# A convolution layer and an eight-expert network: routing by chunks of 2048 tokens, the network in 135 picked units between the convolution's tiles

## The chip, the cores and the metric

The kernel runs on one core of one Trainium2 chip. The metric is the device time of one execution in microseconds, lower being better. The kernel before takes 4087.13 us (median of 3 runs, 4083.84 to 4097.9).

## The reference

Input `x` has 8 images of 256 channels and 64 by 64 pixels, all in float32. A convolution layer is followed by a layer of experts; both add to their input.

```python
# x = x + conv(_ln_c(x));  t = tokens(x);  t = t + ffn(_ln_t(t))
y = depthwise 3x3 of 9 experts; moe = silu(sum_e scale[e,c] * y[e,c] + bias[c])
out = silu(t2 * (w_out @ moe) + shift)
...
idx = argmax(softmax(x @ gate_w + gate_b))        # one expert of 8 for each token
pos = (cumsum(one_hot, axis=0) * one_hot).sum(-1) - 1
kept = pos < C                                    # C = 5120, from 1.25 * 32768 / 8
buf = zeros((E, C, D)).at[idx, pos_safe].set(x, mode='drop')
hmid = relu(einsum('ecd,edf->ecf', buf, w1) + b1) # 256 -> 1024
ybuf = einsum('ecf,efd->ecd', hmid, w2) + b2      # 1024 -> 256
y_tok = ybuf[idx, pos_g] * (prb * kept)[:, None]
y = nan_to_num(y_tok)
```

There are T = 32768 tokens (one for each pixel) and 8 x 5120 = 40960 slots. A token's position is its rank among all tokens of the same expert in the order of the tokens, so a slot is known only when all earlier tokens have been routed. The nine depthwise kernels of a channel collapse to one 3x3 kernel, which both versions compute on the chip (`keff`).

## The kernel before

The kernel is written with a tile framework: it names buffers from pools, and the framework puts the waits in and decides the order of the instructions on each engine's queue. Each engine works through its queue in order. DMAs are issued from the queues of SP (most loads and stores), ACT (the output) and POOL (indirect ones). The kernel has three phases, one behind the other.

**Phase 1** goes over 64 pixel tiles of 512 pixels (8 to an image; 256 channels are two halves of 128 partitions). `norm_stats` and `norm_apply` normalise over channels an image ahead. `conv_taps` makes the 3x3 convolution: TensorE takes four taps as matmuls with diagonal weights (L318), VectorE adds the other five in place in PSUM (L326). `conv_out` is the 1x1 convolution (L340), silu on ACT (L347) and the residual on POOL (L354). `to_tokens` transposes to token-major, writes the tokens to `x_d` in DRAM and computes the gate's logits (L373). Once an image (4096 tokens) is complete, `route_image` turns logits into slots with a chain of small VectorE operations and running counts. `scatter` then writes (token, probability) into the slot table `tab_d` with 32 indirect DMAs from POOL (L474), 128 rows of 8 bytes each. They write the same DRAM tensor, and each waits for the one before it.

**Phase 2** starts when the slot table is complete. It goes over the 8 experts and all 40 slot tiles of 128 of each, whether used or not, in 80 groups of four. For a group it gathers the tokens by the table (L551, POOL), normalises them (L560 to L566), transposes, runs 256 -> 1024 (L587) and 1024 -> 256 (L607) on TensorE, adds the bias on VectorE (L616), multiplies by the probability on ACT (L617), replaces non-finite values (L626 to L633, with POOL's L628) and stores to `y_d`. The weights of an expert, two loads of 1 MB, are loaded once (L541, L543).

**Phase 3** goes over the 64 tiles again: it loads the tokens (L645), gathers the outputs with four indirect DMAs of 128 rows (L651, POOL), adds, transposes back (L664) and stores the result (L673).

Of the kernel before, what the change touches and what calls it, by code (L numbers as in the profile page):

```python
# [8 lines left out]
F32 = mybir.dt.float32  # L9
I32 = mybir.dt.int32  # L10
# [4 lines left out]
DRAM = bass.MemoryType.DRAM  # L15

# [5 lines left out]
# Depthwise taps that the tensor engine takes (diagonal weights); the vector engine adds the rest.  # L22
PE_TAPS = (0, 1, 2, 3)
DVE_TAPS = (4, 5, 6, 7, 8)
# [3 lines left out]
def metaformer_kernel(  # L28
# [26 lines left out]
    NE = w_experts.shape[0]  # conv experts  # L55
# [3 lines left out]
    CAP = max(1, -(-5 * T // (4 * E)))  # ceil(1.25 * T / E)  # L59
    NT = CAP // P  # slot tiles of an expert; slot pos = p * NT + j  # L60
    assert C == D == 2 * P and CAP % P == 0 and w_experts.shape[2:] == (3, 3)
    PX = 512  # pixels of a tile
    RT = PX // W  # image rows of a tile
    NPT = HW // PX  # pixel tiles of an image
    AHEAD = 4  # pixel tiles that loads run ahead of the first use
    NJ = PX // P  # token tiles of a pixel tile
    NIT = HW // P  # token tiles of an image
    NSLOT = E * CAP

    x_v = x.rearrange("b (c p) h w -> b p c (h w)", p=P)  # L70
    out_v = out.rearrange("b (c p) h w -> b p c (h w)", p=P)

    const = ctx.enter_context(tc.tile_pool(name="const", bufs=1))
    dram = ctx.enter_context(tc.tile_pool(name="dram", bufs=1, space=DRAM))

    x1_d = dram.tile([T, C], F32, name="x1_d")  # x after the conv layer, by token
    tab_d = dram.tile([NSLOT, 2], F32, name="tab_d")  # slot -> (token, probability)
    y_d = dram.tile([NSLOT + 1, D], F32, name="y_d")  # expert outputs by slot, then a zero row
# [3 lines left out]
    slots = const.tile([P, B * NIT], I32, name="slots")  # L82

    # The slot table starts at token 0 with probability 0; y_d's last row is 0.
    zeros = const.tile([P, max(NSLOT * 2 // P, D)], F32, name="zeros")
    nc.gpsimd.memset(zeros, 0.0)
    nc.sync.dma_start(
        tab_d.rearrange("(p j) t -> p (j t)", p=P), zeros[:, : NSLOT * 2 // P]
    )
    nc.sync.dma_start(y_d[NSLOT : NSLOT + 1, :], zeros[0:1, :D])  # L90

    b1_sb = const.tile([P, E * NFC], F32, name="b1_sb")

    def rsqrt_eps(dst, var, eps, mhalf):
        nc.gpsimd.tensor_scalar(dst, var, eps, None, ALU.add)
        nc.gpsimd.tensor_tensor(dst, dst, mhalf, ALU.pow)

    # ------------------------------------------------------------------ phase 1
    # Norm over channels, depthwise conv, 1x1 conv, residual, gating, slot table.
    with ExitStack() as ph:  # L100
        wk = ph.enter_context(tc.tile_pool(name="wk1", bufs=1))
        xp = ph.enter_context(tc.tile_pool(name="xp", bufs=18))
        st = ph.enter_context(tc.tile_pool(name="st1", bufs=2))
        io = ph.enter_context(tc.tile_pool(name="io1", bufs=2))
        ps_tr = ph.enter_context(tc.tile_pool(name="ps_tr1", bufs=3, space=PSUM))
        ps_acc = ph.enter_context(tc.tile_pool(name="ps_acc", bufs=3, space=PSUM))
        ps_o = ph.enter_context(tc.tile_pool(name="ps_o1", bufs=1, space=PSUM))
        ps_g = ph.enter_context(tc.tile_pool(name="ps_g", bufs=1, space=PSUM))

        x_tiles = {}  # L110

        def load_x(b, t):
            xt = xp.tile([P, NCC, PX], F32, tag="xt", name="xt")
            nc.sync.dma_start(xt, x_v[b, :, :, t * PX : (t + 1) * PX])
            x_tiles[b, t] = xt

        for t in range(AHEAD):
            load_x(0, t)

        # ---- weights and constants  # L120
        NR = 5 * NE + 4
        rows = wk.tile([NR, C], F32, name="rows")
# [6 lines left out]
        wexp = wk.tile([P, NCC, NE, 9], F32, name="wexp")  # L129
# [3 lines left out]
        wo_sb = wk.tile([P, NCC, C], F32, name="wo_sb")  # L133
        nc.scalar.dma_start(wo_sb, w_out.rearrange("(o p) c -> p o c", p=P))
        wg_sb = wk.tile([P, NCC, E], F32, name="wg_sb")
# [3 lines left out]
        b1_rows = wk.tile([E * NFC, P], F32, name="b1_rows")  # L139
        nc.scalar.dma_start(b1_rows, b1.rearrange("e (f p) -> (e f) p", p=P))  # L140

        mhalf = wk.tile([P, NIT], F32, name="mhalf")
# [3 lines left out]
        cmean = wk.tile([P, P], F32, name="cmean")  # L146
        nc.gpsimd.memset(cmean, 1.0 / C)
        # ntri[k, m] = -1 where k >= m, else 0
# [11 lines left out]
        # erank[e] = E - e  # L160
        erank = wk.tile([P, E], F32, name="erank")
        for e in range(E):
            nc.gpsimd.memset(erank[:, e : e + 1], float(E - e))
        ones_j = wk.tile([P, NIT], F32, name="ones_j")
        nc.gpsimd.memset(ones_j, 1.0)
        count = wk.tile([P, E], F32, name="count")
        nc.gpsimd.memset(count, 0.0)

        par = wk.tile([P, NCC, NR], F32, name="par")
        for c in range(NCC):  # L170
            tr = ps_tr.tile([P, 2, 256], F32, tag="tr", name="tr")
            nc.tensor.transpose(
                tr[:, 0, :NR], rows[:, c * P : (c + 1) * P], ident[:NR, :NR]
            )
            nc.vector.tensor_copy(par[:, c, :], tr[:, 0, :NR])
# [5 lines left out]
        def affine(g, b, m, v, n, name):  # L181
            # t = g * (v + eps)^-0.5, shift = b - m * t
            t = wk.tile([P, NCC, n], F32, name=name + "_t")
            s = wk.tile([P, NCC, n], F32, name=name + "_s")
            mh = wk.tile([P, NCC, n], F32, name=name + "_mh")
            nc.gpsimd.memset(mh, -0.5)
            rsqrt_eps(t, v, BN_EPS, mh)
            nc.vector.tensor_mul(t, t, g)
            nc.vector.tensor_mul(s, m, t)
            nc.vector.tensor_sub(s, b, s)  # L190
            return t, s
# [7 lines left out]
        # The experts' kernels, weighted and summed: one 3x3 kernel per channel.  # L199
# [14 lines left out]
        diag = wk.tile([P, NCC, len(PE_TAPS), P], F32, name="diag")  # L214
        for c in range(NCC):
            for i, k in enumerate(PE_TAPS):
                nc.vector.tensor_scalar(
                    diag[:, c, i, :], ident, keff[:, c, k : k + 1], None, ALU.mult
                )
        woT = wk.tile([P, NCC, C], F32, name="woT")  # L220
        for c in range(NCC):
            tr = ps_tr.tile([P, 2, 256], F32, tag="tr", name="tr")
            for o in range(NCC):
                nc.tensor.transpose(
                    tr[:, 0, o * P : (o + 1) * P],
                    wo_sb[:, o, c * P : (c + 1) * P],
                    ident,
                )
            nc.vector.tensor_copy(woT[:, c, :], tr[:, 0, :C])
        tr = ps_tr.tile([P, 2, 256], F32, tag="tr", name="tr")  # L230
        nc.tensor.transpose(tr[:, 0, : E * NFC], b1_rows, ident[: E * NFC, : E * NFC])
        nc.vector.tensor_copy(b1_sb, tr[:, 0, : E * NFC])
        # (v - mean(v)) @ gate_w = v @ (gate_w - column means of gate_w)
        gm = ps_g.tile([P, NIT * E], F32, tag="g", name="gm")
# [12 lines left out]
        # Normed images with a border of zeros, two in turn.  # L247
        xns = []
        for i in range(2):
            xn = wk.tile([P, NCC, H + 2, W + 2], F32, name=f"xn{i}")  # L250
            nc.gpsimd.memset(xn[:, :, 0 : H + 2 : H + 1, :], 0.0)
            nc.gpsimd.memset(xn[:, :, 1 : H + 1, 0 : W + 2 : W + 1], 0.0)
            xns.append(xn)

        stats = {}

        def norm_stats(b, t):
            xt = x_tiles[b, t]
            mv = st.tile([P, NJ, 2], F32, tag="mv", name="mv", bufs=4)
            for j2 in range(NJ // 2):  # L260
                tr = ps_tr.tile([P, 2, 256], F32, tag="tr", name="tr")
                for jj in range(2):
                    j = 2 * j2 + jj
                    for c in range(NCC):
                        nc.tensor.transpose(
                            tr[:, jj, c * P : (c + 1) * P],
# [3 lines left out]
                for jj in range(2):  # L270
                    s6 = st.tile([P, 6], F32, tag="s6", name="s6", bufs=4)
                    nc.vector.bn_stats(s6, tr[:, jj, :])
                    nc.vector.bn_aggr(mv[:, 2 * j2 + jj, :], s6)
            rs = st.tile([P, NJ], F32, tag="rs", name="rs", bufs=4)
            rsqrt_eps(rs, mv[:, :, 1], LNC_EPS, mhalf[:, :NJ])
            stats[b, t] = mv, rs

        def norm_apply(b, t):
            xn = xns[b % 2]
            xt = x_tiles[b, t]  # L280
            mv, rs = stats.pop((b, t))
            # A transpose of a column spread over 128 columns puts it, as a row, on all
            # partitions.
            bm = ps_tr.tile([P, PX], F32, tag="tr", name="bm")
            br = ps_tr.tile([P, PX], F32, tag="tr", name="br")
            for j in range(NJ):
                nc.tensor.transpose(
                    bm[:, j * P : (j + 1) * P],
                    mv[:, j, 0:1].to_broadcast([P, P]),
# [431 lines left out]
```

## Time and profile before

| what | value |
|---|---|
| runs | 4087.13 us median, 4083.84 to 4097.9 |
| profiled execution: span, first to last instruction | 4073.0 us; no separate time is listed for it, the runs' median is 14.1 us above the span |
| busy: TensorE (PE), VectorE (DVE), ACT, POOL | 85%, 42%, 24%, 35% of the span |
| bytes moved | 273.20 MB, 67 GB/s over the span |
| phase 1 on TensorE | 0 to 1241 us |
| between phases 1 and 2 | 1241 to 1382 us, TensorE busy 0.52 us |
| phase 2 | 1382 to 3708 us, TensorE busy 2297.19 us |
| phase 3 | 3708 to 4073 us, POOL busy 269.54 us |

"PE" is TensorE's matmuls and transposes, "PEld" its weight loads, which overlap. A float32 matmul appears as two instructions in the trace, a transpose as one. "DMA share" is the mean busy share of the core's 16 DMA engines. An engine's idle time is put down to what ended it.

### The profile page before, as it was taken

The page shows a single profiled execution, that of the slowest core. Times are in us where ns is not written, and L with a number is a line of the kernel's source. Part 1 is how long each engine was busy: PE and PEld are TensorE (multiplying, and loading weights), DVE is VectorE, ACT ScalarE, POOL GpSimd, SP SyncE. Part 2 cuts the span into 40 slices and gives each one's busy share as a digit, 9 for nine tenths or more (in the row PEclk, how much of TensorE's full clock was granted, in tenths as well). Part 3 has the DMA queues.
Part 4 walks back from the last instruction along what each step waited for, and adds up shares of the span by engine and source line. Part 5 has one row for each costly group of instructions (what it writes and reads, how often), then busy time and mean ns, then how long its engine had stood idle before and what let it go on. Part 6 is the DMA issues. An engine that isn't in the chain of part 4 may idle for free. (4 is left out here: it accounts for less than half of the span.)

```text
span 4073.0 us, 35799 instructions
## 1 busy us (share of the span) xinstructions
PE 3470.7 (85%) x12971; PEld 2238.5 (55%) x12971; DVE 1724.0 (42%) x3986; ACT 976.3 (24%) x1656; POOL 1438.3 (35%) x1385
## 2 busy tenths in 40 slices
PE   6988888999870499999999999999999999995333
PEld 4554444555440266666666666666666666663232
DVE  7876676777550223232323232333333333322333
ACT  0222122222220123232323232222222222221111
POOL 2244444445433322222222222222222222214776
PEclk9998899999885699999999999999999999997555
DMA  3212121221011111110101111111011111104887
GB/s 111 73 53 57 47 58 52 57 63 37 27 37 49 29 37 38 57 41 32 63 32 42 53 42 45 50 32 63 33 41 56 39 34 39 35 28 156 284 289 272
DMA packets 165972, 273.20 MB, mean 67 GB/s; under 512 B 27058, under 2 KB 102180, under 8 KB 165796
## 3 DMA queue, kind: packets, MB, share of 16 engines
q1 hardware_dynamic: 108194, 160.06, 11.9%
q0 software_dynamic: 35840, 75.81, 6.2%
q10 hardware_dynamic: 21762, 35.05, 2.3%
q8 instruction: 102, 1.67, 0.2%
q14 instruction: 74, 0.61, 0.1%
HBM read 161.20 MB, written 109.64 MB: 66 GB/s over the span
## 5 line engine op out<-in xcount | busy, mean ns | idle before, releaser
L587 PE MATMUL ph_f<-xT,w_sb 128*128 128x512 f32 x2560 | 1121.2, 596 | 23.1 <-ACT xT L582 23.1
L607 PE MATMUL py<-w_sb,hT 128*128 128x256 f32 x5120 | 1118.2, 379 | 0.0
L607 PEld LDWEIGHTS py<-w_sb,hT 128*128 128x128 f32 x5120 | 974.1, 190 | 165.1 <-issue 38.3
L587 PEld LDWEIGHTS ph_f<-xT,w_sb 128*128 128x128 f32 x2560 | 481.0, 190 | 616.3 <-issue 554.6
L551 POOL DMA_INDIRECT xg<-x_d,tab x320 | 319.7, 999 | 1317.8 <-PE tr L577 1238.2
L594 ACT ACTIVATE hT<-ph_f,b_sb 128x512 f32<-128x512 f32 x640 | 439.7, 687 | 642.2 <-PE ph_f L587 642.2
L616 DVE TENSOR_TENSOR v<-py,b_sb 128x256 f32<-128x256 f32 x320 | 121.0, 420 | 1058.0 <-PE py L607 1058.0
L318 PE MATMUL acc<-xn,diag 128*128 128x512 f32 x1024 | 498.2, 628 | 9.3 <-ACT moe L329 9.3
L326 DVE SCALAR_TENSOR_TENSOR acc<-xn,keff,acc 128x512 f32<-128x512 f32 x640 | 444.7, 750 | 57.7 <-PE acc L318 55.4
L474 POOL DMA_INDIRECT tab_d<-dat,slots x256 | 255.9, 1000 | 544.5 <-DMA tab_d<-dat,slots 492.2
L664 PE MATMUL tr<-ident,yt 128*128 128x128 f32 x512 | 120.9, 422 | 244.9 <-issue 159.2
L318 PEld LDWEIGHTS acc<-xn,diag 128*128 128x128 f32 x1024 | 195.2, 202 | 204.3 <-issue 191.6
L651 POOL DMA_INDIRECT yt<-y_d,slots x256 | 269.5, 1053 | 84.4 <-issue 63.1
L340 PE MATMUL po<-moe,woT 128*128 128x512 f32 x512 | 270.9, 653 | 8.7 <-ACT x1c L347 6.9
L617 ACT ACTIVATE v<-v,tab 128x256 f32<-128x256 f32 x320 | 145.1, 502 | 544.9 <-DVE v L616 544.9
L664 PEld LDWEIGHTS tr<-ident,yt 128*128 128x128 f32 x512 | 100.2, 223 | 265.5 <-issue 235.8
L582 ACT COPY xT<-tr 128x512 f32<-128x512 f32 x160 | 92.6, 579 | 621.2 <-PE tr L577 621.2
L560 DVE BATCH_NORM_STATS2 s<-xg 128x6 f32<-128x256 f32 x320 | 131.3, 411 | 255.7 <-DMA xg<-x_d,tab 255.6
L347 ACT ACTIVATE x1c<-po,on_s,on_t 128x512 f32<-128x512 f32 x128 | 99.5, 777 | 543.6 <-PE po L340 543.5
L628 POOL TENSOR_TENSOR alt<-alt,neg 128x1024 f32<-128x1024 f32 x80 | 188.2, 2353 | 99.7 <-DVE neg L627 97.8
L354 POOL TENSOR_TENSOR x1c<-x1c,xt 128x512 f32<-128x512 f32 x128 | 164.9, 1290 | 147.4 <-ACT x1c L347 145.6
L577 PE MATMUL tr<-ident,xg 128*128 128x128 f32 x640 | 84.0, 275 | 140.5 <-DVE xg L566 140.5
(110 smaller groups left out, 2544.7 us busy)
## 6 DMA issues: line engine op xcount, KB each, us to landing
y_d<-alt SPq DMA_DIRECT2D x80, 512.0 KB, 2.6
xt<-in_x SPq DMA_DIRECT2D x64, 512.0 KB, 3.9
x_d<-x1t SPq DMA_DIRECT2D x64, 512.0 KB, 4.2
xr<-x_d SPq DMA_DIRECT2D x64, 512.0 KB, 4.0
out<-oc ACTq DMA_DIRECT2D x64, 512.0 KB, 6.4
w_sb<-in_L_ffn_w SPq DMA_DIRECT2D x16, 1024.0 KB, 8.9
xg<-x_d,tab POOLq DMA_INDIRECT x320, 2.9
tab_d<-dat,slots POOLq DMA_INDIRECT x256, 3.2
```

Of the source, the lines that this page charges most:

```text
L318: nc.tensor.matmul(acc3, lhsT=diag[:, c, i, :], rhs=tap(k), start=(i == 0), stop=(i == len(PE_TAPS) - 1),)
L326: nc.vector.scalar_tensor_tensor(acc3, tap(k), keff[:, c, k : k + 1], acc3, ALU.mult, ALU.add)
L340: nc.tensor.matmul(po, lhsT=woT[:, c, o * P : (o + 1) * P], rhs=moe[:, c, :], start=(c == 0), stop=(c == NCC - 1),)
L354: nc.gpsimd.tensor_add(x1c[:, o, :], x1c[:, o, :], xt[:, o, :])
L474: nc.gpsimd.indirect_dma_start(out=tab_d[:], out_offset=bass.IndirectOffsetOnAxis(ap=sl[:, j : j + 1], axis=0), in_=dat[:, j, :], in_offse ...
L551: nc.gpsimd.indirect_dma_start(out=xg[:, j, :], out_offset=None, in_=x1_d[:], in_offset=bass.IndirectOffsetOnAxis(ap=tab[:, e, j0 + j, 0:1 ...
L587: nc.tensor.matmul(ph_f[:, : n * P], lhsT=w1_sb[:, c, f * P : (f + 1) * P], rhs=xT[:, c, : n * P], start=(c == 0), stop=(c == NCC - 1),)
L594: nc.scalar.activation(hT[:, f, : n * P], ph_f[:, : n * P], AF.Relu, bias=b1_sb[:, e * NFC + f : e * NFC + f + 1],)
L607: nc.tensor.matmul(py[:, jj, :], lhsT=hT[:, f, j * P : (j + 1) * P], rhs=w2_sb[:, f, :], start=(f == 0), stop=(f == NFC - 1),)
L628: nc.gpsimd.tensor_add(al, al, ne)
L651: nc.gpsimd.indirect_dma_start(out=yt[:, j, :], out_offset=None, in_=y_d[:], in_offset=bass.IndirectOffsetOnAxis(ap=slots[:, i : i + 1], a ...
L664: nc.tensor.transpose(tr[:, j * P : (j + 1) * P], yt[:, j, c * P : (c + 1) * P], ident,)
```

## The change

The three phases become two. The kernel goes over the 64 tiles once, in steps; a step normalises tile k + 2, convolves tile k, runs the 1x1 convolution of tile k - 1, runs up to two **units** of the network and makes tokens of tile k - 2. Every four tiles, a chunk of 2048 tokens, it routes (`route`, the same chain of operations on 128 x 128 elements) and scatters the **normalised tokens themselves**, 16 indirect DMAs of 128 rows of 1 KB, to `xs_d` by slot. `pick_units` then takes, on the chip, as many full units of 256 consecutive slots of one expert as the plan allows: none after chunk 0, eight after each of chunks 1 to 14, 23 after chunk 15, 135 in all. A unit becomes due three steps after its chunk's routing. `unit` reads expert and slot from a register (two register loads on SP), then loads its 256 tokens, both weight matrices, both biases, and stores to `y_d`. After the last chunk, `fill_rests` writes zero rows behind the last tokens (16 scatters) and `fill_unused` writes zeros over unused slots of `y_d` (40 indirect DMAs). `finish` is phase 3, with the probability and the replacement of non-finite values moved into it; `x` after the convolution is kept channel-major in DRAM.

In the convolution, the first eight tiles keep four taps on TensorE; the other 56 have all nine on VectorE, in SBUF. The normalisation now multiplies and adds on ACT and is transposed back on TensorE.

The core of the diff, with new functions (line numbers of the new file where the prediction speaks of them):

```diff
-PE_TAPS = (0, 1, 2, 3)
-DVE_TAPS = (4, 5, 6, 7, 8)
...
-    tab_d = dram.tile([NSLOT, 2], F32, name="tab_d")
+    xs_d = dram.tile([NSLOT + U, D], F32, name="xs_d")
...
 def conv_taps(b, t):
+            n_pe = PE_TAPS if b * NPT + t < PE_TILES else 0
...
+                    nc.vector.tensor_scalar(
+                        acc, tap(0), keff[:, c, 0:1], None, ALU.mult)          # L380
+                for k in range(max(1, n_pe), 9):
+                    nc.vector.scalar_tensor_tensor(                           # L384
+                        acc, tap(k), keff[:, c, k : k + 1],
+                        ps if k == n_pe else acc, ALU.mult, ALU.add)
...
+        def scatter(src, idx):
+            nc.gpsimd.indirect_dma_start(                                     # L587
+                out=xs_d[:],
+                out_offset=bass.IndirectOffsetOnAxis(ap=idx, axis=0),
+                in_=src, in_offset=None,
+                bounds_check=NSLOT - 1, oob_is_err=False)
...
+        def unit(ut, i):
+            e = val(0, E - 1)            # register load from ut, L652
+            base = val(1, NSLOT)
+            xs = fp.tile([P, UJ, D], F32, tag="xs", name="xs", bufs=3)
+            nc.sync.dma_start(                                                # L664
+                xs, xs_d[ds(base, U), :].rearrange("(j p) d -> p j d", p=P))
+            w1_sb = fp.tile([P, NCC, FF], F32, tag="w1", name="w1_sb")        # 2 buffers
+            nc.sync.dma_start(                                                # L668
+                w1_sb, w1[ds(e, 1)].rearrange("o (c p) f -> p (o c) f", p=P))
...
+            nc.sync.dma_start(                                                # L674
+                w2_sb, w2[ds(e, 1)].rearrange("o (f p) d -> p (o f) d", p=P))
...
+            for f2 in range(0, NFC, 2):  # L696: 128x256 matmuls, L711 the second layer
...
+            nc.vector.tensor_add(                                             # L719
+                y, py, b2_sb.unsqueeze(1).to_broadcast([P, UJ, D]))
+            nc.sync.dma_start(                                                # L722
+                y_d[ds(base, U), :].rearrange("(j p) d -> p j d", p=P), y)
+
+        def finish(b, t):
+            nc.sync.dma_start(xr, x1_v[b, :, :, px])                          # L731
+            for j in range(NJ):
+                nc.gpsimd.indirect_dma_start(                                 # L734
...
+            for j in range(NJ):
+                nc.scalar.mul(yt[:, j, :], yt[:, j, :], probs[:, i0 + j : i0 + j + 1])
+            nc.vector.tensor_scalar(alt, yt, FLT_MAX, 1e4, ALU.is_gt, ALU.mult)
+            nc.vector.tensor_scalar(neg, yt, -FLT_MAX, 1e4, ALU.is_lt, ALU.mult)
+            nc.gpsimd.tensor_sub(alt, alt, neg)                               # L751
+            nc.vector.tensor_scalar(fin, yt, 0.0, 0.0, ALU.mult, ALU.is_equal)
+            nc.vector.copy_predicated(alt, fin, yt)
...
+        for k in range(-2, N + 3):
+            if (s := at(4)) and s not in x_tiles:
+                load_x(*s)
+            if s := at(2):
+                norm(*s)
+            if s := at(0):
+                moes[s] = conv_taps(*s)
+            if s := at(-1):
+                conv_out(*s, moes.pop(s))
+            for q in [q for q in queue if q[0] <= k][:2]:
+                queue.remove(q)
+                unit(*q[1:])
+            if s := at(-2):
...
+                to_tokens(*s, *chunks[ch])
+                if i == CT - 1:
...
+                    route(ch, rs, lg)
+                    for t4, tn in enumerate(tns):
+                        for j in range(NJ):
+                            scatter(tn[:, j, :], slots[:, i0 : i0 + 1])
+                    if plan[ch]:
...
+                        if last:
+                            fill_rests(tot, nb)
+                            fill_unused(nb)
+                        queue += [(k + LAG, *u) for u in pick_units(plan[ch], nb)]
+        for q in queue:
+            unit(*q[1:])
+        for s in steps:
+            finish(*s)
```

## The prediction, made before the result was known

> **What bounds the kernel now.** I read the stages first, then what ends POOL's waits, then the rows that the change multiplies. The stages, cut where TensorE's work changes (stage, its length, busy us of PE, PEld, DVE, ACT, POOL, granted clock, DMA share, GB/s):
>
> ```profile
> 0.00:1241.00 1241.00, 1052.15 (x4139) 607.87 (x4139) 864.64 (x2172) 277.90 (x472) 522.67 (x532) 0.92 0.19 56
> 1241.00:1382.00 141.00, 0.52 (x2) 0.18 (x1) 5.83 (x20) 0.00 (x0) 47.44 (x50) 0.50 0.16 44
> 1382.00:3708.00 2326.00, 2297.19 (x8320) 1530.25 (x8319) 733.46 (x1665) 661.56 (x1120) 598.65 (x548) 1.00 0.13 42
> 3708.00:4073.00 365.00, 120.86 (x512) 100.22 (x512) 120.02 (x131) 36.81 (x64) 269.54 (x256) 0.55 0.79 275
> ```
>
> Phase 2 is TensorE alone, 2297 of 2326 us. Phase 1 is mixed: 1241 / 64 = 19 us a tile. In the 141 us between them only POOL works, on the last scatters. The timeline there (start, duration, POOL, [idle before and its releaser]):
>
> ```profile
> 1349.85 0.97 POOL L474 DMA_INDIRECT tab_d<-dat,slots  x1 [2.64 <-DMA tab_d<-dat,slots]
> 1352.72 0.97 POOL L474 DMA_INDIRECT tab_d<-dat,slots  x1 [1.90 <-DMA tab_d<-dat,slots]
> 1355.35 0.97 POOL L474 DMA_INDIRECT tab_d<-dat,slots  x1 [1.66 <-DMA tab_d<-dat,slots]
> 1358.28 0.97 POOL L474 DMA_INDIRECT tab_d<-dat,slots  x1 [1.96 <-DMA tab_d<-dat,slots]
> ```
>
> Each scatter waits for its predecessor to land. From 1280.65 to 1360.66 there are 27 steps, **2.96 us each**. With two 1 MB weight loads in flight, near 1250, a step took 6 to 7 us. Phase 3's gathers don't wait so: 0.95 + 0.30 us each, and 359 / 64 = 5.6 us a tile in all. The rows that I price with:
>
> ```profile
> L607 PE MATMUL py<-w_sb,hT 128*128 128x256 f32 x5120 | 1118.2, 379 | 0.0
> L326 DVE SCALAR_TENSOR_TENSOR acc<-xn,keff,acc 128x512 f32<-128x512 f32 x640 | 444.7, 750 | 57.7 <-PE acc L318 55.4
> L628 POOL TENSOR_TENSOR alt<-alt,neg 128x1024 f32<-128x1024 f32 x80 | 188.2, 2353 | 99.7 <-DVE neg L627 97.8
> L96 POOL TENSOR_TENSOR rs<-rs,mhalf 128x4 f32<-128x4 f32 x152 | 193.8, 1275 | 12.4
> L354 POOL TENSOR_TENSOR x1c<-x1c,xt 128x512 f32<-128x512 f32 x128 | 164.9, 1290 | 147.4 <-ACT x1c L347 145.6
> ```
>
> Matmuls overlap, so pace and not mean counts: the timeline has 64 of L607 in 13.98 us, 0.215 us for 256 columns.
>
> [...] 128 KB scatters should keep nearly the same step. [...]
>
> **The change part by part.**
>
> *Network.* A unit is 64 matmuls at 0.215 plus four transposes at 0.13: 14.3, taken as 14.4 us. 135 x 14.4 = 1944 instead of 2326 us: 382 us less on TensorE. The weights are loaded 135 times: about 2.5 MB loaded and 0.26 stored per unit, 194 GB/s if units stand back to back. Phase 3 shows 275, so I hide it under the matmuls; if the cover fails, see rival B. [...]
>
> *Convolution.* TensorE loses 56 x 16 matmuls at 0.43 = 385 us. VectorE gets 16 taps at 0.69 and two cheaper ones at 0.41 a tile, 11.9 us instead of 10 x 0.75. A tile leaves TensorE 3.4 us of 1x1 convolution, 24 transposes (3.1) and 16 gate matmuls (3.2): 9.8 us. A chunk then asks TensorE for 8 x 14.4 + 4 x 9.8 = 154 us, VectorE for about 82 (four tiles at 16.7, routing, picking, eight bias additions), POOL for 38. If all overlapped, TensorE would be the bound.
>
> *The new wait.* It doesn't all overlap. I looked at the order of the changed kernel's instructions on each queue. In every chunk, the first unit's load of `xs` (L664) behind a routing waits for the **last of the 16 scatters**, because both touch one DRAM tensor at addresses known only at run time. On SP, that unit's weight loads (L668, L674) are queued behind the waiting load; on TensorE, all later units and tiles stand behind the unit, except one normalisation and two to three 1x1 convolutions, some 12 us. So a chunk has a serial piece. From the end of the unit before:
>
> - last token tile and logits: transposes 0.5, gate matmuls 3.2, statistics and a power on POOL (1.28 + 0.25) beside them: **5 us**
> - routing: about 25 VectorE operations; 12 at 0.28 [...], eight scans at 0.2, the rest 5: 10 us. Its queue mixes in 10 or 16 taps, in turns; 13 x 0.69 = 9. **19 us**
> - 16 scatters at 2.96, and 2 for POOL's additions (1.29) and powers in between: **49 us**
> - `xs` issued, register load, first weight load (a lone 1 MB load of before landed in 5.0 us): **7 us**
>
> That is 80 us, then 8 x 14.4 = 115, the tile work not already done, 39 - 12 = 27, and three places where TensorE waits through a chain of statistics, POOL's power, ACT and transposes (about 6 us each, 18): **240 us a chunk** instead of 154. For the serial piece I have ends of 65 and 105 us (scatter steps of 2.4 and 4; the trace's fastest was 2.37), so 225 to 265.
>
> *Sum.* Thirteen such cycles lie between the routings of chunks 2 and 15.
>
> - Start: 31 us of set-up (first L318 at 31.3) and 14 tiles at today's 19, VectorE being as loaded as before on average, plus 13 for the part of the first four units that shows: 310
> - 13 x 240 = 3120
> - After the last chunk: 24 to route; 16 scatters and 16 of `fill_rests`, the 40 zero writes mixed in between (each in the other's wait), 32 x 3.0 = 97; 7; the remaining 27 units, 389: 517
> - `finish`: POOL's 5.6 us a tile get 2.35 for the subtraction that moves here: 64 x 8.0 = 512, and 13 to drain: 525. Today 365. VectorE (about 5 us a tile), ACT (2) and DMA are under that.
>
> 310 + 3120 + 517 + 525 = 4472, against the profiled span of 4073. The runs' median lies 14 above the span, so **4486 us**. The two kernels would be even at **209 us a cycle**: (4073 - 1352) / 13. The 382 us saved, the 141 us gap and the shorter phase 1 are all in this sum; the serial pieces, 80 us thirteen times, and `finish` take them back.
>
> **The rivals.**
>
> *A, faster.* The scatters don't wait for each other (or land faster than the next is issued). Then they run in the gathers' rhythm, 16 x 1.25 + 3 = 23 instead of 49 us, and with POOL free sooner half of the 18 us of chain waits goes: 205 a cycle, 2665 in all, **4031 us**. It decides as soon as the serial piece and the waits lose 31 us together. For it: phase 3 shows POOL issuing every 1.25 us. Against it: the timeline above, with one tensor written in the same way, and the changed order, where each scatter has its predecessor's semaphore in front.
>
> *B, the weights.* 2 MB per unit come late: 8.9 us was the median landing of a 1 MB load (5.0 to 12.8), and an `xs` or `w2` row is 1 KB. With 3 us lost per unit, 4486 + 135 x 3 = **4890 us**. Against it: each load is issued one unit and a half, 21 us, ahead of use.
>
> *C, POOL's order.* The additions and powers between scatters wait for inputs that are late, and the scatters behind them too: 70 instead of 49 us, 261 a cycle, **4759 us**. For it: L354 waited 145.6 us for ACT.
>
> That too few full units exist can't be: 2048 tokens a chunk less at most 8 x 255 left over give the plan's numbers.
>
> **How the numbers follow.** My forecast 0.58, its own range 4310 to 4680 (cycle 228 to 255, other terms 30). A 0.14, B 0.13, C 0.15. The range for 8 in 10 takes C and most of B, and on the low side a mild form of A: **4150 to 4850**. Faster by over 0.3% (what a measurement of this kernel can tell from no change) 0.15, within it 0.02, slower 0.83.
>
> **What would show it.** Right: L587 at about 3 us a step, released by its own DMA; 13 to 14 holes of 60 us or more in TensorE's row, ended by L664 or L668; VectorE under half busy; a `finish` of 8 us a tile led by POOL. Wrong: TensorE over 85% busy in the middle (A); matmuls L696 and L711 waiting for weight loads in every unit (B); scatters released by DVE or ACT (C); a `finish` at 5.6 us a tile.

## The result, and the profile after

| | before | after |
|---|---|---|
| median of the runs, us | 4091.2 (4083.8 to 4097.9, 4 runs) | 4549.4 (4541.1 to 4556.0, 4 runs) |
| span of the profiled execution, us | 4073.0 | 4549.6 |

The ratio of after to before is 1.1121, with a 95% interval of 1.1101 to 1.1141. The changed kernel is 458 us slower.

The slices on the page of the changed kernel (the span in 40 parts of 114 us; each digit is the busy share in tenths, PEclk the granted TensorE clock in tenths):

```profile
PE   6757575858494948484848494958583699812222
PEclk9868787979696969697969797878786799955555
```

Where the kernel before has one long phase at nearly full TensorE, there is now a comb: from slice 10 to slice 25 (counted from 0) TensorE is under half busy in every other one. The granted clock follows: 6 or 7 tenths in those slices, 8 or 9 in the ones between. Only the tail (slices 32 to 34) is dense. Cut at the routing of chunk 2, the routing of chunk 15, the first gather of `finish` and the end, the stages are (length, busy us of PE, PEld, DVE, ACT, POOL, granted clock, DMA share, GB/s):

```profile
0.00:439.00 439.00, 287.41 (x1084) 180.86 (x1084) 242.45 (x636) 143.17 (x264) 148.16 (x158) 0.83 0.24 77
439.00:3457.00 3018.00, 2107.70 (x9561) 1712.38 (x9562) 968.22 (x2480) 825.94 (x1717) 519.71 (x507) 0.82 0.38 122
3457.00:3969.00 512.00, 392.50 (x1842) 342.70 (x1842) 23.74 (x65) 105.24 (x243) 70.20 (x72) 0.88 0.51 167
3969.00:4550.00 581.00, 121.93 (x512) 99.59 (x512) 349.15 (x384) 129.45 (x256) 411.12 (x320) 0.53 0.51 166
```

The second row holds 13 cycles: 3018 / 13 = **232.1 us a chunk** (the routing matmul L496 starts at 439.0 and at 3456.8). TensorE is busy 70% of it, VectorE 32%. In the last row POOL is the busiest engine. What TensorE waited for, over the whole run (total us, times, longest):

```profile
PE tr L683 <- DMA xs<-xs_d: 625.9, 15, 108.9
...
PE tr L351 <- ACT xk L341: 226.5, 61, 8.2
```

The first row is the new wait: a unit's token transposes, 15 times, 42 us on average. SP, which issues the loads, waits for the scatters ahead of L664:

```profile
SPq L664 <- DMA xs_d<-tn,slots: 416.3, 14, 37.9
```

The timeline of the changed kernel shows one of them (start, duration, engine, [idle before and its releaser]; scatters of the middle left out):

```profile
1566.76 7.07 PE L696 MATMUL ph<-xT,w_sb 128*128 128x256 f32 x32
...
1587.48 7.07 PE L711 MATMUL py<-w_sb,hT 128*128 128x256 f32 x32
...
1617.37 1.10 POOL L587 DMA_INDIRECT xs_d<-tn,slots  x1 [7.73 <-DVE ucum L551]
...
1632.77 7.04 POOL L587 DMA_INDIRECT xs_d<-tn,slots  x1 [1.70 <-DMA xs_d<-tn,slots]
...
1663.44 0.97 POOL L587 DMA_INDIRECT xs_d<-tn,slots  x1 [1.70 <-DMA xs_d<-tn,slots]
1666.11 0.97 POOL L587 DMA_INDIRECT xs_d<-tn,slots  x1 [1.70 <-DMA xs_d<-tn,slots]
...
1668.55 0.39 SPq L664 DMA_DIRECT2D xs<-xs_d  x1
...
1671.40 1.09 PE L683 MATMUL tr<-ident,xs 128*128 128x128 f32 x4 [31.28 <-DMA xs<-xs_d]
...
1676.06 10.03 PE L696 MATMUL ph<-xT,w_sb 128*128 128x256 f32 x32 [3.57 <-DMA w_sb<-in_L_ffn_w]
```

Read it from the bottom. The unit's first layer starts at 1676.06, and its last 3.57 us of waiting were for its weights. Its tokens were transposed at 1671.40. They were loaded at 1668.55, when the last of 16 scatters, issued at 1666.11, had landed. Each scatter takes 0.97 us of POOL and then waits 1.70 us for its own predecessor's DMA: a step of 2.67 us. The unit before ended near 1594 (L711), so the serial piece is 1676 - 1594 = **82 us**.

### The profile page after: what moved, and what is told of

Its sections match the earlier page's. It is cut to its first block, busy times and chain, and to the rows that moved or that the text cites. A ratio compares the mean times of both kernels' runs of the same rounds, so it can differ in the third digit from the quotient of the medians.

```text
span 4549.6 us, 38799 instructions
## 1 busy us (share of the span) xinstructions
PE 2909.5 (64%) x12997; PEld 2335.5 (51%) x12997; DVE 1583.6 (35%) x3564; ACT 1203.8 (26%) x2480; POOL 1149.2 (25%) x1057
## 5 line engine op out<-in xcount | busy, mean ns | idle before, releaser
L696 PE MATMUL ph<-xT,w_sb 128*128 128x256 f32 x4320 | 1003.1, 392 | 56.4 <-DMA w_sb<-in_L_ffn_w 50.9
L711 PE MATMUL py<-w_sb,hT 128*128 128x256 f32 x4320 | 954.4, 379 | 0.0
L696 PEld LDWEIGHTS ph<-xT,w_sb 128*128 128x128 f32 x4320 | 845.1, 197 | 192.0 <-issue 56.1
L711 PEld LDWEIGHTS py<-w_sb,hT 128*128 128x128 f32 x4320 | 820.8, 190 | 111.6
L384 DVE SCALAR_TENSOR_TENSOR moe<-xn,keff,moe 128x512 f32<-128x512 f32 x960 | 698.7, 779 | 110.8 <-ACT xn L354 108.8
L705 ACT ACTIVATE hT<-ph,b_sb 128x256 f32<-128x256 f32 x1080 | 452.9, 470 | 954.7 <-issue 482.7
L683 PE MATMUL tr<-ident,xs 128*128 128x128 f32 x540 | 118.4, 362 | 625.9 <-DMA xs<-xs_d 625.9
L308 POOL TENSOR_SCALAR rsc<-mv 128x4 f32<-128x4 f32 x64 | 17.0, 266 | 1969.5 <-DVE mv L307 1969.4
L587 POOL DMA_INDIRECT xs_d<-tn,slots x256 | 323.3, 1263 | 488.5 <-DMA xs_d<-tn,slots 341.2
L351 PE MATMUL tr<-ident,xk 128*128 128x128 f32 x512 | 135.1, 398 | 227.3 <-ACT xk L341 226.5
L418 POOL TENSOR_TENSOR xt<-so,xt 128x512 f32<-128x512 f32 x128 | 184.6, 1443 | 248.1 <-ACT so L411 247.5
L351 PEld LDWEIGHTS tr<-ident,xk 128*128 128x128 f32 x512 | 77.5, 192 | 300.5 <-ACT xk L341 295.1
L306 DVE BATCH_NORM_STATS2 s<-tr 128x6 f32<-128x256 f32 x512 | 199.6, 414 | 60.5 <-PE tr L322 60.2
```

Of the source, the lines that this page charges most:

```text
L306: nc.vector.bn_stats(s6, src(j))
L351: nc.tensor.transpose(tr[:, j * P : (j + 1) * P], xk[:, j, c * P : (c + 1) * P], ident)
L384: nc.vector.scalar_tensor_tensor(acc, tap(k), keff[:, c, k : k + 1], ps if k == n_pe else acc, ALU.mult, ALU.add,)
L418: nc.gpsimd.tensor_add(xt[:, o, :], so[:, o, :], xt[:, o, :])
L587: nc.gpsimd.indirect_dma_start(out=xs_d[:], out_offset=bass.IndirectOffsetOnAxis(ap=idx, axis=0), in_=src, in_offset=None, bounds_check=NS ...
L683: nc.tensor.transpose(tr[:, c * U + j * P : c * U + (j + 1) * P], xs[:, j, c * P : (c + 1) * P], ident,)
```

## The experiments

The theory: a cycle is set by a serial piece (routing, then a chain of 16 scatters, then the load of the tokens), because TensorE's next unit stands behind the scatters. Rivals: late weights, the order on POOL, VectorE's taps. A second theory concerns `finish`: POOL's subtraction leads it.

**1. Twice the scatters (e2_double).** In the loop after `route`:

```
 scatter(tn[:, j, :], slots[:, i0 : i0 + 1])
+scatter(tn[:, j, :], slots[:, i0 : i0 + 1])
```

> The changed kernel with each token scatter issued twice in a row, same rows to the same slots: 32 scatters a chunk instead of 16. Theory (each scatter waits for its predecessor to land, and the chain of 16 lies wholly on the path): a step of 2.67 us, measured from 1617.37 to 1666.11, makes 16 x 2.67 = 43 us more a cycle; 13 cycles, the tail once and one or two chunks of the start: 15 x 43 = 640 us more, 5130 to 5230 us. Rival A (POOL's issue of about 1 us sets the pace): 16 x 1.0..1.25 x 15 = 240 to 300 us more. Rival (the last tile's and the routing's work on VectorE sets the hole, scatters lie beside it): under 100 us more.

Measured: 5198 us (5188 to 5208), 649 more than the changed kernel, and a cycle of (4047.1 - 491.2) / 13 = 273.5 us, 41.4 more. TensorE's waits in this kernel:

```profile
PE tr L683 <- DMA xs<-xs_d: 1268.8, 15, 157.4
```

The wait grew by 643 us and the kernel by 649 (637 in span). The chain lies wholly on the path: 41.4 / 16 = 2.6 us for each added scatter, near the step of 2.67 that its landing sets, not the 0.97 of POOL's issue.

**2. Token loads ahead of the next chunk's scatters (e1_xs_ahead).** Four of a chunk's eight units are still queued when the next chunk is routed. Their tokens have long been complete, but their loads stand behind scatters that don't concern them.

```
                 if i == CT - 1:
                     tns, rs, lg = chunks.pop(ch)
+                    for q in queue:
+                        early[id(q[1]), q[2]] = load_xs(q[1], q[2])
                     route(ch, rs, lg)
...
-            xs = fp.tile([P, UJ, D], F32, tag="xs", name="xs", bufs=3)
+            xs = fp.tile([P, UJ, D], F32, tag="xs", name="xs", bufs=5)
...
-    xp = ctx.enter_context(tc.tile_pool(name="xp", bufs=8))
+    xp = ctx.enter_context(tc.tile_pool(name="xp", bufs=7))
```

> The changed kernel with one thing added: right before a chunk is routed, the token loads (xs, L664) of the four units still queued are issued, so that they no longer stand behind the 16 scatters of that chunk; xs gets 5 buffers instead of 3 and the x pool 7 instead of 8. Theory (the serial piece of a cycle is the wait of already complete units for scatters that don't concern them): four units, 4 x 14.7 us = 59 us, can now run while the routing and the scatters go on, so a cycle falls from 232.1 us to 173-190 and the tail loses up to as much once: 4550 - 14 x 42..59 = 3720 to 3960 us; TensorE's wait for xs (625.9 us in 15 places) falls under 150. Rival B' (the loads are late because of the weights or of DMA bandwidth): the wait moves to the weight loads of L696 and L711, less than 100 us gained. Rival C' (the chain of a tile on POOL and VectorE sets the cycle): cycle stays above 215, less than 250 us gained.

Measured: 4096 us, ratio to the kernel before 1.0003 (0.9992 to 1.0013): level with it, 453 us better than the changed kernel. The cycle is 197.9 us, which misses the 173 to 190 expected, and the tail lost only 18 us, not 59. TensorE's waits here (the token transposes are now L692):

```profile
...
PE tr L351 <- ACT xk L341: 389.9, 61, 22.5
...
PE tr L692 <- DMA xs<-xs_d: 90.0, 2, 64.8
```

The wait for tokens is gone but for two, and weights don't appear in its place. The edit also gives `xs` more buffers, but in the changed kernel it was the scatters' DMA that ended SP's wait before L664, not a buffer. Of the 536 us freed there, 163 came back before L351, the transposes of a normalised tile. The timeline of the same kernel:

```profile
1693.44 0.97 POOL L587 DMA_INDIRECT xs_d<-tn,slots  x1 [5.54 <-DMA xs_d<-tn,slots]
...
1703.69 0.30 DVE L307 BATCH_NORM_AGGREGATE mv<-s 128x2 f32<-128x6 f32 x2
...
1716.35 0.97 POOL L587 DMA_INDIRECT xs_d<-tn,slots  x1 [1.72 <-DMA xs_d<-tn,slots]
...
1717.39 0.23 POOL L308 TENSOR_SCALAR rs<-mv 128x4 f32<-128x4 f32 x1
1717.70 1.04 POOL L309 TENSOR_TENSOR rs<-rs,mhalf 128x4 f32<-128x4 f32 x1
...
1719.67 1.15 PE L351 MATMUL tr<-ident,xk 128*128 128x128 f32 x4 [17.05 <-ACT xk L341]
```

The tile's statistics are ready at 1704, but its power waits on POOL until the last scatter is issued, and TensorE loses 17.05 us. Some of the scatters are also slower (a wait of 5.54 instead of 1.70 us); what slows them was not tried. This is the prediction's rival C in another place: it matters once the larger wait is gone.

**3. The taps back on TensorE (e3_pe_taps).**

```
-        PE_TILES = 8
+        PE_TILES = 64
```

> The changed kernel with the taps undone: four of the nine taps of every tile on TensorE again, as in the kernel before (PE_TILES 64). It puts 56 x 16 matmuls of 0.43 us = 385 us of work back on TensorE and takes about 56 x 6 us off VectorE. Theory 1 (TensorE idle in the hole and in chain waits, and the tile work stands partly in the hole's shadow): of the 385 us only the tiles that don't lie in the hole show, three of four: +200 to +330 us, 4750 to 4880 us. Theory 2 (VectorE's taps are what holds POOL's scatters and the tiles' pace): fewer taps from SBUF shorten the start by 50 us or more, the scatters of 7 to 23 us vanish (longest L587 under 5 us), and the kernel is within 100 us of 4550 or faster. If TensorE bound the kernel, all of +385 would show.

Measured: 4718 us, 169 more; a cycle of 245.9 us. Both theories miss. Moving the taps off TensorE is worth less than half of its 385 us. The hole takes most of the rest: the wait for tokens fell from 625.9 to 427.2 us, so some 199 us of the added work only filled idle time. Theory 2 is right on one point alone. The scatters of both kernels, changed and then this one (duration in ns min/median/max, first and last start):

```profile
L587 POOL DMA_INDIRECT xs_d<-tn,slots x256: 969/971/23085, 171.8 to 3509.4; - x128
```
```profile
L587 POOL DMA_INDIRECT xs_d<-tn,slots x256: 966/972/1387, 171.7 to 3675.3; - x128
```

The longest went from 23 us to 1.4 us, yet the routing of chunk 2 came only 8 us earlier (430.7 instead of 439.0), no more than kernels with the same start differ by (433.8 in experiment 4, 442.0 in the plain kernel of experiment 5). The long scatters are not what made the start long.

**4. `finish`'s subtraction on VectorE (e4_sub_dve).**

```
-            nc.gpsimd.tensor_sub(alt, alt, neg)
+            nc.vector.tensor_sub(alt, alt, neg)
```

> The changed kernel with the subtraction of finish (L751, 2.35 us on POOL) put on VectorE; nothing else. Theory (finish goes at POOL's pace: four gathers of 1.25 and a subtraction of 2.35 us a tile, and a gap behind it because two tiles run in step): finish falls from 581 to 350-430 us, in all 4320 to 4400 us. Rival (DMA bandwidth or latency of gathers sets finish): under 40 us gained. Rival (VectorE becomes its bound, with about 7 us a tile): 64 x 7 = 450 us, 4420 us.

Measured: 4432 us (4416 to 4449, two runs 33 us apart), 117 less. In the trace, which is of the slower run, `finish` takes 4447 - 3964 = 483 us. That misses the theory's 350 to 430. The last rival comes near with its number (450 us, 4420 in all) but not with its reason: VectorE was busy 351 of the 483 us, POOL 389. POOL has no subtraction left and still needs 7.5 us a tile. Its timeline says why:

```profile
4199.99 0.70 DVE L752 TENSOR_SCALAR neg<-yt 128x1024 int32<-128x1024 f32 x1
4200.02 4.40 POOL L734 DMA_INDIRECT yt<-y_d,slots  x1 [0.30 <-issue]
4200.59 0.71 DVE L749 TENSOR_SCALAR alt<-yt 128x1024 f32<-128x1024 f32 x1
4201.19 1.31 DVE L753 COPY_PREDICATED alt<-neg,yt 128x1024 f32<-128x1024 int32 x1
4202.38 1.23 DVE L751 TENSOR_TENSOR alt<-alt,neg 128x1024 f32<-128x1024 f32 x1
```

One gather stays on POOL for 4.40 us, while VectorE works from SBUF to SBUF: it ends at 4204.42, 0.81 us after the last operation shown. A gather of 0.95 us would have been over before L753 began, so L752 and L749, with one input each, have held it too. The mean gather of this kernel took 1.52 us instead of the changed kernel's 1.02.

**5. What holds the gathers.** Three kernels without the clean-up in `finish`: one plain (e7_no_nan), one with two-input operations on VectorE beside the gathers (e8_tt), one with one-input operations (e9_ts).

```
-            nc.vector.tensor_scalar(alt, yt, FLT_MAX, 1e4, ALU.is_gt, ALU.mult)
...
-            nc.vector.copy_predicated(alt, fin, yt)
+            for _ in range(3):                      # second kernel only
+                nc.vector.tensor_sub(alt, yt, yt)
+            for _ in range(5):                      # third kernel only
+                nc.vector.tensor_scalar(alt, yt, FLT_MAX, 1e4, ALU.is_gt, ALU.mult)
```

> The changed kernel without the clean-up of infinite and undefined values in finish: L749 to L753 are left out (their part of the computation is not done) and the transposes read yt. POOL has the gathers alone, VectorE only the additions from PSUM. Theory (finish goes at POOL's pace, and POOL's issue is held while VectorE works from SBUF to SBUF): every gather takes 0.95 us and the pace is that of the kernel before, 5.0 to 5.6 us a tile: 64 x 5.0..5.6 + 13 = 333 to 371 us instead of 581, 4300 to 4345 us in all. Rival (the DMA of gathers, loads and stores sets it): over 420 us of finish.

> e7_no_nan with three VectorE subtractions a tile (128x1024 fp32, both inputs from SBUF, about 1.22 us each, result unused, nobody waits for them): 3.7 us a tile of VectorE work beside the gathers. The question is which kind of VectorE operation holds POOL's indirect DMA issue. If operations with two inputs from SBUF hold it: the mean L734 goes from 0.95 to 1.3 us or more (up to 3.7 / 4 more each), finish to 64 x 6..8.5 us. If only operations [...] hold it (L749: 0.69 us for 1024 elements): L734 stays at 0.95 to 1.0.

> e7_no_nan with five VectorE compare-and-multiply operations a tile (L749's form, 128x1024 fp32, one input from SBUF, 0.69 us each, result unused, nobody waits for them): 3.5 us a tile beside the gathers. If operations with one input [...] hold POOL's issue: the mean L734 goes from 0.95 to 1.3 us or more. If only two inputs from SBUF hold it: L734 stays at 0.95 to 1.0, and finish at that of e7_no_nan.

Measured: 4296 us, just under what was expected, 4383 and 4320 us (the last two from one run each). The gathers in the plain kernel, beside two-input operations, and beside one-input operations:

```profile
L734 POOL DMA_INDIRECT yt<-y_d,slots x256: 945/949/1008, 3967.1 to 4286.7; - x128
```
```profile
L734 POOL DMA_INDIRECT yt<-y_d,slots x256 | 326.8, 1277 | 438.0 <-DMA y_d<-y 360.3
```
```profile
L734 POOL DMA_INDIRECT yt<-y_d,slots x256 | 258.5, 1010 | 438.3 <-DMA y_d<-y 360.6
```

Alone, a gather takes 0.95 us, never more than 1.01, and `finish` takes 329 us, 5.1 a tile: DMA did not limit it at 9.06. The other two rows, from the groups of the page, give busy us and mean ns. Beside nearly the same total of VectorE work (192 operations of 1.22 us, 320 of 0.74: 234 and 238 us), two-input operations add 0.33 us to the mean gather, one-input ones 0.06 us. Both are a little off what was expected (1.3 us or more; 0.95 to 1.0). Chance of place is no rival: 225 gathers of the second kernel and 240 of the third overlap such an operation. At 3.7 us of such work a tile, the two-input kind costs 85 us of span, the other 22. So both kinds held POOL here, the two-input kind much more.

**6. Both mendings together (e5_both).** The edits of experiments 2 and 4 in one kernel.

> e1_xs_ahead and e4_sub_dve together: token loads of the queued units ahead of the scatters, and finish's subtraction on VectorE. If the two places are independent, their gains in span add up: 4549.6 - 466.0 (e1) - 102.4 (e4) = 3981 us, about 100 us under the kernel before: ratio 0.970 to 0.978. If e4's gain in finish depends on what ran before, or VectorE's subtraction meets the tail, 4000 to 4060.

Measured: 3962 us (3931 to 3965); ratio to the kernel before 0.960 (0.957 to 0.963), a little better than expected. The span, 3962.7, is 18 us under the sum of the two gains, less than the 33 us between the two runs of experiment 4. So nothing speaks against the two places being independent.

**7. POOL's order, first try (e6_spread).** The scatters written eight by eight into the two steps that follow:

```
-                            scatter(tn[:, j, :], slots[:, i0 : i0 + 1])
+                            late.append((tn[:, j, :], slots[:, i0 : i0 + 1]))
...
+            for a in late[:8]:
+                scatter(*a)
+            del late[:8]
```

> e5_both with the 16 scatters of a chunk issued eight by eight in the two steps that follow (behind the convolution's POOL work of each step) instead of all at once behind the routing. In e1_xs_ahead TensorE's wait for xs is gone, and the longest one of a cycle (17.05 us at 1719.67, before L351) stands for the power L308/L309 of the next tile, which is queued behind the 16 scatters on POOL. Theory (rival C of the prediction, POOL's order, is what bounds once the wait for xs is gone): that wait shrinks to the 2 to 5 us of the other tiles, a cycle goes from 198 to 178-186 us: 13 x 12..20 = 150 to 260 us less than e5_both, 3720 to 3830 us. Rival 1 (the wait only moves: every tile's statistics stand behind eight scatters): no more than 50 us less than e5_both. Rival 2 (TensorE's own work, 154 to 160 us a chunk, and the weight loads set the cycle already): no more than 50 us either, with TensorE over 88% busy in the middle.

Measured: 3969 us (3938 to 3973), the same as without. This looks like rival 1, but it is no test. The timeline has the last scatter ahead of L308, and L351 waits 17.05 us as before:

```profile
1715.93 0.97 POOL L587 DMA_INDIRECT xs_d<-tn,slots  x1 [1.71 <-DMA xs_d<-tn,slots]
1716.97 0.23 POOL L308 TENSOR_SCALAR rs<-mv 128x4 f32<-128x4 f32 x1
```

POOL's order comes from a scheduler; the edit changed no dependence, and nothing had moved.

**8. POOL's order, by a true dependence (e10_late).** The last eight indices of a chunk (the last two chunks excepted) are copied by an operation that also reads a later tile's `rs`:

```
+                rs = norm(*s)
+                if late and k >= late[0][2]:
+                    sl = st.tile([P, 2 * NJ], I32, tag="sl", name="sl")
+                    nc.vector.scalar_tensor_tensor(
+                        sl, rs[:, 0:1].to_broadcast([P, 2 * NJ]), 0.0,
+                        slots[:, i0 : i0 + 2 * NJ], ALU.mult, ALU.add)
+                    for i, (tn, _, _) in enumerate(late):
+                        scatter(tn, sl[:, i : i + 1])
```

> e5_both with the second eight scatters of a chunk made to depend on a later tile's power: their indices are copied on VectorE (128x8, plus 0 times that tile's rs), so that the order on POOL becomes eight scatters, the power L308/L309 that L351 waits for, then eight scatters. In e6_spread the new place in the program changed nothing of POOL's order: the timeline still had all 16 scatters ahead of that power, and the wait of 17.05 us before L351. Theory (POOL's order is what bounds next): that wait falls to 2 to 6 us, a cycle from 198 to 184-188 us, 13 x 10..14 = 130 to 180 us less than e5_both in span: 3780 to 3830 us. Rival (the wait only moves: the later scatters now end later, and the next chunk's token loads or the next tile's statistics wait for them instead): within 40 us of e5_both's 3963.

Measured: 3800 us (3779 to 3821); ratio to the kernel before **0.924 (0.919 to 0.929)**. The cycle is (2848.4 - 456.4) / 13 = 184.0 us. In the timeline the power now has scatters on both sides:

```profile
1604.95 0.97 POOL L588 DMA_INDIRECT xs_d<-tn,slots  x1 [1.79 <-DMA xs_d<-tn,slots]
...
1624.18 0.23 POOL L308 TENSOR_SCALAR rs<-mv 128x4 f32<-128x4 f32 x1 [18.26 <-DVE mv L307]
...
1626.41 1.10 POOL L588 DMA_INDIRECT xs_d<-tn,sl  x1 [0.87 <-DVE sl L789]
...
1626.47 1.14 PE L351 MATMUL tr<-ident,xk 128*128 128x128 f32 x4 [3.76 <-ACT xk L341]
```

L351 waits 3.76 instead of 17.05 us, and over the whole run 206.4 instead of 393.9 us; POOL stands idle for 18.26 us before the power. Of the 13 x 14.1 = 183 us that the cycles gain over experiment 6, the start gives back 19 (chunk 2 is routed at 456.4 instead of 437.3). That the first chunks' later scatters delay the first units is my reading and was not tried.

## Why the prediction was right, and where it was off

It said 4486 us, and 4549 was measured, for the reason that it named. Term by term:

| term | predicted | measured | off by |
|---|---|---|---|
| start, until the last token tile of chunk 2 | 310 | 419 | +109 |
| 13 cycles | 3120 | 3018 | -102 |
| tail, until the last unit's end | 517 | 529 | +12 |
| `finish`, from there | 525 | 584 | +59 |

(The routing of chunk 2 was at 439 and I take 20 us off for what lies ahead of it in a cycle, as the prediction did. The bounds are thus 419, 3437, 3966 and 4550. The last unit ahead of chunk 15's routing ended near 3445; counted from there, the tail is 521 us.)

That the sum came so near is in part luck: a start that is 109 us too long stands against cycles that are 102 us too short. The four terms miss by 78 us together, and the 14 us added for the runs' median were not there (4549.4 against a span of 4549.6).

**The cycle's step held.** The serial piece was priced at 80 us. The one shown is 82, and those of chunks 3 to 14 take 78.6 to 81.5, 80 on average (from the last L711 ahead of the wait to the first L696 behind it). Inside it errors cancel: the scatter's step is 2.67 us, with 128 KB in each, rather than the 2.96 that scatters of 1 KB took before, but in every other cycle one scatter takes 7 us, and here the piece from 1617.37 to 1668.55 is 51 us where 49 was written. The register loads take 0.27 us each here (median of 270). A tap goes at a pace of 0.67 us (10.01 us for 15 of L384; priced at 0.69), a cheaper one at 0.44 (0.87 us for two of L380; priced at 0.41), and a 128x128 routing operation takes 0.28 (L468, the mean of 16), as priced; no row of before stood behind the two prices of a tap. What was too dear is TensorE's three waits in a cycle, priced at 6 us each, which are 5.15, 3.42 and 2.17 us before L351 (at 1477.81, 1519.07 and 1561.75): 11 instead of 18. What has no term is the clock: from 1617 to 1669 the granted clock was 0.53, and the first 32 matmuls of the unit behind took 10.03 us, where 32 of them had taken 7.07 before the hole.

So the first twelve cycles took 234.9 us on average instead of 240. The thirteenth took 198.5 (routings at 3258.2 and 3456.8), because the tiles ran out: the last was normalised by 3207, and its 1x1 convolution ended at 3268. The prediction has thirteen equal cycles; the short one makes up 3 of the 8 us by which the mean of 232.1 lies lower. Experiment 1 shows the chain of scatters on the path; experiment 2 shows that undoing this one wait takes the loss back.

**The start was mis-sized.** The failing step is "14 tiles at today's 19, plus 13 for the part of the first four units that shows". Up to chunk 0's routing the pace was right (168 us, where the term implies 165). The four tiles to chunk 1's routing took 103 us instead of 76, and the four to chunk 2's, with four units among them, 168 instead of 89: 79 us more, near the four units in full (4 x 14.4 = 58 us) and the hole of 25.1 us for the first `xs` ahead of them. The price of 13 assumed the units mostly hidden; that they show in full is read from this sum and was not tried. Why the four tiles before took 26 us each stays open: experiment 3 gives VectorE fewer taps and gains 3 us there, experiment 1 doubles chunk 0's scatters and loses 5, so neither seems to be the main part.

**`finish` was mis-sized.** The step "5.6 us get 2.35 for the subtraction" treats POOL's work as a sum of its parts, with VectorE, ACT and DMA "under that". It gives 8.0, but 581 / 64 = 9.1 us a tile. A pair of tiles has eight gathers (10 us), two subtractions (4.65) and then a gap. The timeline of the changed kernel:

```profile
4208.11 4.65 POOL L751 TENSOR_TENSOR alt<-alt,neg 128x1024 f32<-128x1024 f32 x2
...
4210.50 2.82 DVE L752 TENSOR_SCALAR neg<-yt 128x1024 int32<-128x1024 f32 x1 [6.38 <-POOL alt L751]
...
4213.35 1.29 DVE L753 COPY_PREDICATED alt<-neg,yt 128x1024 f32<-128x1024 int32 x1
...
4215.42 1.23 POOL L734 DMA_INDIRECT yt<-y_d,slots  x1 [2.66 <-issue]
```

VectorE's L752 takes 2.82 us beside POOL's subtraction (0.69 is the median of all), L753 follows it, and POOL's next gather starts 2.66 us late. The trace names no engine for this gap, but its place does. `yt` has six buffers (`bufs=6`), so a tile's gathers need the buffer of six tiles before, which VectorE reads last in L753. There are 27 such gaps, 71.9 us in all, one for each pair from the eleventh tile on. In 26 of them the first gather starts 0.76 to 0.78 us after L753 of exactly six tiles before has ended. In experiment 4, where POOL no longer subtracts, that L753 has ended at least 15.5 us before, and no gather starts late. So POOL waits for a buffer that VectorE frees, and VectorE has waited for POOL's subtraction: 1.1 us a tile that no sum of one engine's work contains. A kernel with more buffers was not run.

**The rivals.** A fell: the scatters wait for each other. B fell: the first layer waited for weights 50.9 us in 14 times, 3.6 each. C was not needed for this result (of the 489 us for which POOL waited ahead of the scatters, their own DMA ended 341, and the statistics of a tile, L307, 63), but experiments 2 and 8 show that it was next in line at 14 us a cycle. VectorE stayed under half busy, as said; the hole before a unit is shorter than the 60 us foretold, 38 us on average over the 13 cycles ((625.9 - 108.9 - 25.1) / 13), because tile work falls into the middle of the serial piece (from 1617 to 1669 TensorE was busy 9.8 us). In the whole piece of 82 us TensorE stood idle for 59.

## What to carry to other kernels

Here work was produced in chunks through one DRAM tensor with run-time addresses, and a load behind a chunk's stores waited for them, needed or not (416.3 us of SP's waits, 14 times). In such a kernel, issue the loads of complete data before the next chunk's stores. That one move was worth 453 us here, nearly all of the 458 that the change had lost. Price the buffers too: in `finish`, VectorE, less busy than POOL (349 us against 411), still decided when a buffer came free, and that cost 72 us. When a long wait goes, look at once at which engine's queue holds the next one, and if a scheduler sets the order, check the order in the trace before reading the time: experiment 7 would have passed for a refutation.

## What the hardware showed that was not expected

POOL's issue of an indirect DMA was held here while VectorE ran operations with two inputs from SBUF, once for 23.09 us. In the start of the changed kernel, VectorE and POOL:

```profile
312.69 10.01 DVE L384 SCALAR_TENSOR_TENSOR moe<-xn,keff,moe 128x512 f32<-128x512 f32 x15
...
323.41 10.68 DVE L384 SCALAR_TENSOR_TENSOR moe<-xn,keff,moe 128x512 f32<-128x512 f32 x16
...
334.81 6.70 DVE L384 SCALAR_TENSOR_TENSOR moe<-xn,keff,moe 128x512 f32<-128x512 f32 x10
```
```profile
312.92 1.48 POOL L587 DMA_INDIRECT xs_d<-tn,slots  x1 [0.18 <-issue]
316.34 1.25 POOL L587 DMA_INDIRECT xs_d<-tn,slots  x1 [1.94 <-DMA xs_d<-tn,slots]
319.27 23.09 POOL L587 DMA_INDIRECT xs_d<-tn,slots  x1 [1.69 <-DMA xs_d<-tn,slots]
344.06 0.97 POOL L587 DMA_INDIRECT xs_d<-tn,slots  x1 [1.71 <-DMA xs_d<-tn,slots]
```

A scatter of 0.97 us took 23.09: it ended at 342.36, 0.85 us after the last tap. Six more scatters, one in every other cycle like that at 1632.77, took 7.04 or 7.05 us, and each ended 0.84 us after the last tap of its row. But the two scatters ahead of the long one passed in 1.48 and 1.25 us with taps running; what decides stays open.

In experiment 5 the two-input subtraction held the gathers more (a mean of 1.277 us) than the one-input compare (1.010). One subtraction also takes longer than one compare (1.22 us against 0.74), and no run tells the number of inputs and the length of an operation apart.
